# Graph score rows spread by a DRAM round trip instead of TensorE transposes, with a new table of planner aims

## The chip, the cores and the metric

The kernel runs on one core of a Trainium2 chip. The metric is device time in microseconds of the whole launch. PE is TensorE's matmul side and PEld its weight loads, DVE is VectorE, ACT is ScalarE, POOL is GpSimd, and SP is SyncE, which only issues DMAs here.

## The reference, cut to what matters

Sixteen graphs of 1024 nodes with 256 features go through two layers. Layer 0 is attention with 8 heads, masked by the adjacency; layer 1 applies graph attention twice, and then a feed-forward block. The graph attention is the part that the change touches:

```python
def _gat(h, adj, W, a, out_features):
    Wh = h @ W
    Wh1 = Wh @ a[:out_features]              # one score per node (row)
    Wh2 = Wh @ a[out_features:]              # one score per node (column)
    e = leaky_relu(Wh1 + swapaxes(Wh2, 1, 2), 0.2)
    att = softmax(where(adj > 0, e, NEG), axis=1)
    return att @ Wh
```

`e[i, j]` depends on a number of row i and a number of row j alone. The kernel has j on the partitions and i along the free axis, so the 1024 numbers `Wh1[i]` have to stand as a line that is the same on all 128 partitions.

## The kernel before, in words

All in float32. A planner written in the kernel, the class `Order`, decides in which order instructions are issued on each engine. The work is written as threads (generators) that yield the cost of their next instruction in nanoseconds, such as `on(PE=460)` or `load()`; they take and give buffers of counted pools, and wait for and fire events. The planner goes through all threads at build time and puts, of those instructions that could start within 300 ns of the first one, the one with the smallest `aim` next. Aims are due times, computed from two tables of constants: `AIM`, and `EARLY` for the first two graphs, in units of `SLOT`. The order is then fixed: on the chip every engine runs its list strictly in order and waits for semaphores. SP's list of DMAs is such a list too.

The work of one graph b:

- `mask_part` turns the adjacency into a float8 mask; `x_pair`, `qk_part` (L492, L495, L497) and `v_part` (L524) make transposed inputs, queries and keys (stored to DRAM as high and low halves, L504) and values. They are done for graph b+1 while graph b is in its heads. `load_stacks` (L581) loads the queries and keys of a head from DRAM on SP's queue, into two buffers.
- `all_scores` and `weights`: for every head 8 tiles of scores, in pairs. PE writes a pair (L615, four matmuls) into the two PSUM buffers `ps_s`; for each tile ACT scales it (L631), DVE takes the larger of both (L633), which frees the PSUM buffer, ACT takes the exponential (L636), and POOL multiplies by the mask (L640). `join` (L699, DVE) adds tiles for the row sums. `all_values` is the product with the values on PE (L655). Because there are only two `ps_s` buffers, PE's next L615 pair waits for both L633 of the pair before it.
- `rest`: row norms, L792 to L829 in `rows_pair` (projection, norm, then the product L824 that yields the rows of `Wh` and both scores; ACT copies the rows, L827, DVE copies the two scores into the small tile `check`, L829).
- `attention` runs twice per graph, s = 0 and s = 1. `first_half` makes half of the line: four transposes of a score column that is read as if it were repeated over 128 columns (L860), into one of three `misc` PSUM buffers, and two exponentials on ACT (L862, L864) into the tile `first`. Then `attend` makes eight tiles `att` on DVE, each with L877 (product and maximum), L880 (mask and sum) and L883 (reciprocal), and ACT scales a row block by the reciprocal (L885). Every `attend` needs both halves of `first`. The products that follow, L915 for s = 0 (`second_rows`, which gives the rows and scores for s = 1 by L923 and L925) and L940 for s = 1 (`normed_pair`), need all eight `att` tiles.
- `feed_forward`: L980 and L1008 on PE, evacuated by ACT L989 or DVE L986, then norms on DVE (L350, L352, L1019, L1021) and the store of the result. It can be done late, so that the planner uses it to fill PE in the following graph.

All of this is `unshifted_path`. A second path, `general_path`, is branched to at the end only where sums or scores left a safe range, and isn't executed with these inputs.

In the steady part, one graph takes one slot: 32 score pairs with the values, both graph attentions, and the feed-forward of an earlier graph, all interleaved.

Of the kernel before, what the change touches and what calls it, by code (L numbers as in the profile page):

```python
# [9 lines left out]
FT = mybir.dt.float32  # L10
# [4 lines left out]
AF = mybir.ActivationFunctionType  # L15
OP = mybir.AluOpType

ALPHA = 0.2
EPS = 1e-5
H = 8  # L20
P = 128
HALF = 512
# [164 lines left out]
def on(shared=False, delay=0.0, mode=None, **costs):  # L187
    return "on", (costs, shared, delay, mode)
# [6 lines left out]
def wait(event):  # L195
    return "wait", event
# [6 lines left out]
def take(pool):  # L203
    return "take", pool


def give(pool):
    return "give", pool


def start(thread, aim):
    return "start", (thread, aim)


def aim(time, lead):
    return "aim", (time, lead)
# [17 lines left out]
def unshifted_path(  # L234
# [8 lines left out]
    nc = tc.nc  # L243
    B, N, D = x.shape
    NT = N // P
# [6 lines left out]
    TPH = HALF // P  # L252
# [7 lines left out]
    YW = D + 2  # L260
    NSUM = NT * H + 2 * NT
    NSCORE = 4 * NT
    SLOT = 253e3
    PACE = SLOT / (H * NT // 2)


    AIM = dict(mask0=0.602, x=1.454, x_step=-0.0104, mask=0.9396, mask_step=-0.0101, qk0=0.4907, qk1=1.7441,
               qk_step=-0.0518, v0=0.7416, v1=0.621, v_step=0.0547, rows=-0.079, rows_step=-0.0113, first0=0.2137,
               first1=-0.446, graph0=-0.0793, graph1=0.316, graph_step=0.0481, second=0.7493, second_step=-0.015,
               normed=1.0223, normed_step=-0.0115, ff_wait=(None, 0, 1, 0), ff=(0.5532, 0.1074, 3.6996, 1.0353),  # L270
               ff_step=0.0063, fast0=0.2312, fast1=0.6979, fast15=1.0127, lead=14.8372)

    EARLY = dict(x=2.6481, x_step=-0.1001, mask=0.5019, mask_step=0.0795, qk0=0.7532, qk1=1.2626, qk_step=-0.1325,
                 v0=0.2134, v1=1.5023, v_step=-0.0416, rows=-2.7213, rows_step=-0.3343, first0=-0.8482,
                 first1=-4.695, graph0=0.0441, graph1=-0.9035, graph_step=-0.1073, second=0.463,
                 second_step=0.0554, normed=0.7744, normed_step=0.0342, ff_wait=(None, 0, 1, 0),
                 ff=(2.0875, 0.7055, 1.5112, 0.6358), ff_step=0.0607)

    const = ctx.enter_context(tc.tile_pool(name="const", bufs=1))
    sb = ctx.enter_context(tc.tile_pool(name="sb", bufs=1))  # L280
# [2 lines left out]
    dram = ctx.enter_context(tc.tile_pool(name="dram", bufs=3, space=bass.MemoryType.DRAM))  # L283
# [4 lines left out]
    def share(b, name):  # L288
        return (EARLY if b < 2 else AIM)[name]

    def misc(dtype=FT):
        return psum.tile([P, HALF], dtype, tag=f"misc{work.slot['misc']}", name="ps_m", bufs=1)

    def buf(shape, tag, name, dtype=FT):
        return sb.tile(shape, dtype, tag=tag, name=name, bufs=bufs[tag])


    ident = const.tile([P, P], FT, name="ident")
# [40 lines left out]
    def load(n=1, latency=3500):  # L339

        return on(SP=500 * n, delay=latency)
# [62 lines left out]
    def mask_part(b, t, halves):  # L404

        n = len(halves)
        ints = []
        if b:
            yield take("adj")
        elif halves[0]:  # L410
            yield wait(("mask", b, t, 0))
        for kh in halves:
            yield take("pair")
            ai = buf([P, HALF], "pair", "adj_i", I32)
            ints.append(ai)
            part = adj[b].rearrange("(u p i) k -> u i p k", p=P, i=2)[t // 2, t % 2, :, kh * HALF:(kh + 1) * HALF]
            if b:
                yield pause(1500)
                yield on(ACT=400, delay=3500)
                nc.scalar.dma_start(ai, part)  # L420
            else:
                yield pause(2000)
                yield load()
                nc.sync.dma_start(ai, part)
        yield take("adjb")
        ab = buf([P, 2 * HALF], "adjb", "adj_b", F8)
        for i, ai in enumerate(ints):
            yield on(DVE=336, shared=True)
            nc.vector.tensor_scalar(ab[:, i * HALF:(i + 1) * HALF], ai, 0.0, -1.0,
                                    op0=OP.is_gt, op1=OP.mult, saturate=False)  # L430
            yield give("pair")
        if b:
            yield give("adj")
        yield take("misc")
        pt = misc(BF)
        pairs = ab.bitcast(BF)
        yield on(PE=30 + 140 * n)
        for i in range(2 * n):
            nc.tensor.transpose(pt[:, i * P:(i + 1) * P], pairs[:, i * P:(i + 1) * P], ident_b)
        yield give("adjb")  # L440
        yield on(ACT=46 + 218 * n)
        k0 = 2 * halves[0]
        nc.scalar.copy(masks[b].bitcast(BF).rearrange("p (k q) -> p k q", k=NP)[:, k0:k0 + 2 * n, t * P:(t + 1) * P],
                       pt[:, :2 * n * P].rearrange("p (k q) -> p k q", k=2 * n))
        yield give("misc")
        for kh in halves:
            yield fire(("mask", b, t, kh))

    def make_mask(b, t0):
        yield take("mask")  # L450
        masks[b] = buf([P, NT * N], "mask", "mask", F8)
        parts = [(t, (kh,)) for kh in range(NH) for t in range(NT)] if b == 0 else [(t, (0, 1)) for t in range(NT)]
        for n, (t, halves) in enumerate(parts):
            yield start(mask_part(b, t, halves),
                        t0 + ((share(b - 1, "mask") if b else AIM["mask0"]) + share(b - 1, "mask_step") * n) * SLOT)

# [20 lines left out]
    def qk_part(b, g, o, nh):  # L477

        w = (wq, wk)[o]
        cols = slice(nh * HALF, (nh + 1) * HALF)  # L480
        for u in range(nh * 2, nh * 2 + 2):
            yield wait(("xT", b, u))
        if b:
            yield take("stage")
        yield take("pair")
        yield take("pair")
        yield take("misc")
        pa = misc()
        high, low = (buf([P, HALF], "pair", n) for n in ("high", "low"))
        yield on(PE=1728)  # L490
        for dc in range(DC):
            nc.tensor.matmul(pa, w[:, dc, g * P:(g + 1) * P], xTs[b][:, dc, cols],  # L492
                             start=(dc == 0), stop=(dc == DC - 1))
        yield on(ACT=466)
        nc.scalar.copy(high.bitcast(FR), pa)  # L495
        yield on(DVE=594)
        nc.vector.tensor_tensor(low, pa, high, op=OP.subtract)  # L497
        yield give("misc")
        if (b, g) == (0, 1):

            yield wait(("stack", 0, 0))
        yield load(2)
        for i, part in enumerate((high, low)):
            nc.sync.dma_start(scratch[b, g][o, :, i, cols], part)  # L504
        yield give("pair")
        yield give("pair")
        if b:
            yield give("stage")
        yield fire(("qk", b, g, o, nh))

    def project_qk(b, g, t0):
        scratch[b, g] = dram.tile([2, P, 2, N], FT, name="qk_halves")
        for o in range(2):
            for nh in range(NH):
                yield start(qk_part(b, g, o, nh), t0 + (2 * o + nh) * share(b - 1, "qk_step") * SLOT)

# [20 lines left out]
    def project_v(b, g, t0):  # L537
        yield take("v")
        vs[b, g] = buf([P, NT, G * DH], "v", "v")
        for u in range(NP):  # L540
            yield start(v_part(b, g, u), t0 + share(b - 1, "v_step") * u * SLOT)

# [6 lines left out]
    def project(b, t0):  # L549
        yield take("xT")  # L550
        xTs[b] = buf([P, DC, N], "xT", "xT")
        for u in range(NP):
            yield start(x_pair(b, u), t0 + (share(b - 1, "x") + share(b - 1, "x_step") * u if b else 0.0) * SLOT)
        yield start(make_mask(b, t0), t0 + (0.5 if b else 0.0) * SLOT)
        for g in range(H // G):
# [32 lines left out]
    checks = {}  # L588
    begin = {}

    def pace(b):
        return PACE * {0: AIM["fast0"], 1: AIM["fast1"], B - 1: AIM["fast15"]}.get(b, 1.0)

    def all_scores():
        for b in range(B):
# [4 lines left out]
            for h in range(H):  # L600
                yield wait(("stack", b, h))
                q, kk = stacks[b, h]
                for t in range(NT):
                    due = t0 + (h * NT + t) / 2 * pace(b)
                    if b == 0 or t % 2 == 0:
                        yield aim(due, AIM["lead"] * PACE)
                        for _ in range(2 if b else 1):
# [123 lines left out]
    def scores_of(b, s):  # L731

        c = NSUM + s * 2 * NT
        return checks[b][:, c:c + 2 * NT].rearrange("p (t s) -> p t s", s=2)

    def head_stats(b, q):
        got = yield from stats([hn[b][:, q * TPH + i, :] for i in range(TPH)])
# [112 lines left out]
    def first_half(b, s, nh):  # L850

        first, ac = firsts[b, s], scores_of(b, s)
        cols = slice(nh * HALF, (nh + 1) * HALF)
        for t in range(nh * TPH, (nh + 1) * TPH):
            yield wait(("row", b, s, t))
        yield take("misc")
        pt = misc()
        yield on(PE=460)
        for i in range(TPH):
            nc.tensor.transpose(pt[:, i * P:(i + 1) * P], ac[:, nh * TPH + i, 0:1].to_broadcast([P, P]), ident)  # L860
        yield on(ACT=478)
        nc.scalar.activation(first[:, 0, cols], pt, AF.Exp)  # L862
        yield on(ACT=478)
        nc.scalar.activation(first[:, 1, cols], pt, AF.Exp, scale=ALPHA)  # L864
        yield give("misc")
        yield fire(("first", b, s, nh))

    def attend(b, s, big, rows, j, second, sums):
# [616 lines left out]
```

## Time and profile before

| | |
|---|---|
| times of the runs | 4314.66, 4314.74, 4316.35 us (median 4314.74) |
| profiled execution: its own time, its span | 4317.81 us, 4315.9 us |
| PE busy (share of the span) | 4189.7 us (97%) |
| DVE busy | 3544.8 us (82%) |
| ACT busy | 2942.7 us (68%) |
| POOL busy | 2571.6 us (60%) |
| mean granted TensorE clock | 0.990 |
| DMA traffic | 344.79 MB, 80 GB/s on average |

Busy time is the union of an engine's instructions; the group rows of the profile add up their own instructions, and neighbours on PE overlap because matmuls are pipelined. What ended an idle time is named behind it. A row such as `DVE L633 ... [0.53 <-ACT p L631]` of the timeline says that DVE stood idle for 0.53 us before it, until ACT had done L631.

### The profile page before, as it was taken

The numbers are of one execution on the slowest core, as the hardware profiler recorded it, in microseconds if no ns is written. First come the engines' busy times: TensorE is split into PE (matmuls) and PEld (weight loads), VectorE is DVE, ScalarE is ACT, GpSimd is POOL, SyncE is SP. The second block draws the span as 40 slices with busy tenths as digits, with TensorE's granted clock in tenths as the row PEclk, the third lists the DMA queues.
The fourth block names the chain that finished last, engine by engine and source line by source line (L and its number), as shares of the span: only waits on it lengthen the run. The fifth ranks groups of instructions, "written<-read, shape, count | busy, mean of one in ns | idle before, by whom it ended". The sixth has DMA issues, their size and how long they took to land.

```text
span 4315.9 us, 76274 instructions
## 1 busy us (share of the span) xinstructions
PE 4189.7 (97%) x30027; PEld 3030.3 (70%) x30027; DVE 3544.8 (82%) x5491; ACT 2942.7 (68%) x4362; POOL 2571.6 (60%) x1161
## 2 busy tenths in 40 slices
PE   8788999999999999999999999999999999999999
PEld 4466677677777777777777777777777777777687
DVE  6878878888888887879879788887889879788853
ACT  6756677777767677776776767677776776767632
POOL 5846467664757656574664757646575674747700
PEclk9999999999999999999999999999999999999999
DMA  6413223322232322323232222322323222222100
GB/s 188 125 54 99 69 76 87 91 72 86 74 94 67 96 84 68 90 71 89 84 84 81 79 81 79 91 73 81 91 74 89 81 84 84 74 79 57 30 20 21
DMA packets 156282, 344.79 MB, mean 80 GB/s; under 512 B 21750, under 2 KB 24332, under 8 KB 155916
## 3 DMA queue, kind: packets, MB, share of 16 engines
q1 hardware_dynamic: 112140, 260.13, 21.0%
q10 hardware_dynamic: 43776, 79.71, 6.6%
q8 instruction: 239, 3.92, 0.4%
q14 instruction: 127, 1.04, 0.1%
HBM read 239.09 MB, written 100.66 MB: 79 GB/s over the span
## 4 chain that ended last, share of the span: by engine, by line
PE 82%; DVE 11%; ACT 3%; POOL 1%; DMA 1%; issue 1%; SPq 0%; ACTq 0%; POOLq 0%; DVEq 0%
PE ps_a L655 17%; PE ps_s L615 11%; PE ps_m L915 10%; PE ps_m L980 9%; PE ps_m L940 9%; PE ps_m L1008 7%; PE ps_m L492 4%; DVE p L633 3%; PE ps_m L792 3%; PE ps_m L824 3%; PE ps_m L795 3%; PE ps_m L524 2%; PE ps_m L372 2%; DVE p L699 2%; POOL p L640 1%; DVE att L880 1%
## 5 line engine op out<-in xcount | busy, mean ns | idle before, releaser
L640 POOL TENSOR_TENSOR p<-p,mask 128x1024 f32<-128x1024 f32 x1024 | 2471.1, 2431 | 1425.5 <-ACT p L636 1044.1
L633 DVE TENSOR_TENSOR p<-p,ps_s 128x1024 f32<-128x1024 f32 x1024 | 1211.3, 1213 | 251.2 <-ACT p L631 248.1
L636 ACT ACTIVATE p<-p 128x1024 f32<-128x1024 f32 x1024 | 1082.2, 1059 | 302.3 <-DVE p L633 276.7
L631 ACT ACTIVATE p<-ps_s 128x1024 f32<-128x1024 f32 x1006 | 986.3, 1021 | 345.2 <-PE ps_s L615 283.0
L615 PE MATMUL ps_s<-qs,ks 128*128 128x512 f32 x2048 | 658.7, 437 | 30.6 <-DVE p L633 27.0
L655 PE MATMUL ps_a<-p,v 128*32 128x256 f32 x8192 | 561.9, 388 | 24.4 <-POOL p L640 24.3
L615 PEld LDWEIGHTS ps_s<-qs,ks 128*128 128x128 f32 x2048 | 352.6, 190 | 266.1 <-issue 114.8
L940 PE MATMUL ps_m<-y,att 128*128 128x256 f32 x2048 | 481.1, 382 | 12.6 <-ACT y L885 11.1
L915 PE MATMUL ps_m<-y,att 128*128 128x258 f32 x2048 | 477.1, 383 | 14.4 <-ACT y L885 12.9
L980 PE MATMUL ps_m<-rT,wf 128*128 128x256 f32 x2048 | 474.3, 383 | 9.4 <-ACT hid L989 4.3
L1008 PE MATMUL ps_m<-wf,hid 128*128 128x256 f32 x2048 | 475.7, 381 | 0.6 <-DVE hid L986 0.6
L915 PEld LDWEIGHTS ps_m<-y,att 128*128 128x128 f32 x2048 | 385.5, 190 | 89.3 <-ACT y L885 13.8
L980 PEld LDWEIGHTS ps_m<-rT,wf 128*128 128x128 f32 x2048 | 381.0, 190 | 85.9 <-issue 14.3
L699 DVE TENSOR_TENSOR p<-p 128x1024 f32<-128x1024 f32 x256 | 410.5, 1604 | 23.6 <-PE ps_a L655 23.4
L940 PEld LDWEIGHTS ps_m<-y,att 128*128 128x128 f32 x2048 | 378.4, 190 | 71.1 <-ACT y L885 11.3
L1008 PEld LDWEIGHTS ps_m<-wf,hid 128*128 128x128 f32 x2048 | 379.1, 190 | 63.6 <-issue 8.2
L655 PEld LDWEIGHTS ps_a<-p,v 128*32 128x32 f32 x8192 | 209.5, 109 | 289.3 <-issue 130.8
L655 PE MATMUL ps_a<-p,minus_ones 128*32 128x256 f32 x6144 | 405.8, 382 | 1.2 <-DVE p L699 1.2
L877 DVE SCALAR_TENSOR_TENSOR att<-first,second 128x1024 f32<-128x1024 f32 x256 | 359.7, 1405 | 32.4 <-ACT first L864 28.3
L880 DVE SCALAR_TENSOR_TENSOR att<-mask,att 128x1024 f32<-128x1024 fp8e4 x256 | 339.5, 1326 | 5.6
L655 PEld LDWEIGHTS ps_a<-p,minus_ones 128*32 128x32 f32 x6144 | 199.1, 111 | 138.3 <-issue 7.9
L885 ACT ACTIVATE y<-y,check 128x258 f32<-128x258 f32 x256 | 131.1, 512 | 220.4 <-DVE check L883 217.9
(101 smaller groups left out, 4330.0 us busy)
## 6 DMA issues: line engine op xcount, KB each, us to landing
qs<-qk_halves SPq DMA_DIRECT2D x256, 256.0 KB, 4.0
ks<-qk_halves SPq DMA_DIRECT2D x256, 256.0 KB, 5.2
adj_i<-in_adj_dram ACTq DMA_DIRECT2D x240, 256.0 KB, 3.1
qk_halves<-high SPq DMA_DIRECT2D x128, 256.0 KB, 2.8
qk_halves<-low SPq DMA_DIRECT2D x128, 256.0 KB, 3.6
xr<-in_x_dram ACTq DMA_DIRECT2D x64, 256.0 KB, 4.7
x_kept<-x SPq DMA_DIRECT2D x64, 256.0 KB, 2.0
x<-x_kept SPq DMA_DIRECT2D x64, 256.0 KB, 5.1
```

The lines of the kernel that those rows point to most:

```text
L615: nc.tensor.matmul(ps[:, cols], kk[:, t * P:(t + 1) * P], q[:, cols], start=True, stop=True)
L631: nc.scalar.activation(p, ps, AF.Copy, scale=ALPHA)
L633: nc.vector.tensor_tensor(p, p, ps, op=OP.max)
L636: nc.scalar.activation(p, p, AF.Exp)
L640: nc.gpsimd.tensor_tensor(p, p, mask_of(b, t), op=OP.mult)
L655: nc.tensor.matmul(acc[i * DH:(i + 1) * DH, at:at + QN].rearrange("d (t r) -> d t r", r=DH), w, p.rearrange("k (t i r) -> k i t r", i=4, r ...
L699: nc.vector.tensor_tensor(ps[to], ps[to], ps[by], op=OP.add)
L880: nc.vector.scalar_tensor_tensor(e, mask_of(b, j), -1.0, e, op0=OP.mult, op1=OP.mult, accum_out=sums[:, j:j + 1])
L915: nc.tensor.matmul(pa[:, cols:cols + width], big[:, j, i * P:(i + 1) * P], rows[:, j, :width], start=(j == 0), stop=(j == NT - 1))
L940: nc.tensor.matmul(pa[:, i * D:(i + 1) * D], big[:, j, t * P:(t + 1) * P], y2[:, j, :D], start=(j == 0), stop=False)
L980: nc.tensor.matmul(pa[:, i * 2 * P:(i + 1) * 2 * P], wf1[:, dc, hc * P:(hc + 1) * P], rT[:, dc, :], start=(dc == 0), stop=(dc == DC - 1))
L1008: nc.tensor.matmul(pa[:, i * D:(i + 1) * D], hid[hc // 2][:, hc % 2, i * P:(i + 1) * P], wf2[:, hc, :], start=(hc == 0), stop=False)
```

## The change

The four transposes and their PSUM buffer are gone. SP stores the four score columns of a half, 128 partitions x 4 numbers, to a line of 512 numbers in DRAM, and then loads this line back with a partition step of zero, so that every one of 128 partitions receives it in a tile `raw` of the `pair` pool. The exponentials read `raw` in SBUF. In `check` the first and second scores of a graph now lie in two blocks instead of alternating. `SLOT` and nearly all constants of `AIM` and `EARLY` are new, so that the planner puts nearly all instructions of the program in another order. In the changed program, lines from `first_half` on stand three lines lower (L877 is L880 there, and so on); the text keeps the numbers of the kernel before.

```diff
-    SLOT = 253e3
+    SLOT = 251e3
     PACE = SLOT / (H * NT // 2)
-    AIM = dict(mask0=0.602, x=1.454, x_step=-0.0104, mask=0.9396, mask_step=-0.0101, qk0=0.4907, qk1=1.7441,
-               qk_step=-0.0518, v0=0.7416, v1=0.621, v_step=0.0547, rows=-0.079, rows_step=-0.0113, first0=0.2137,
-               first1=-0.446, graph0=-0.0793, graph1=0.316, graph_step=0.0481, second=0.7493, second_step=-0.015,
-               normed=1.0223, normed_step=-0.0115, ff_wait=(None, 0, 1, 0), ff=(0.5532, 0.1074, 3.6996, 1.0353),
-               ff_step=0.0063, fast0=0.2312, fast1=0.6979, fast15=1.0127, lead=14.8372)
+    AIM = dict(mask0=0.0973, x=3.4713, x_step=0.2368, mask=0.8043, mask_step=-0.0042, qk0=-0.2028, qk1=3.8613,
+               qk_step=-0.1291, v0=0.5183, v1=0.0617, v_step=0.1189, rows=-0.9474, rows_step=0.0512, first0=0.1622,
+               first1=-0.0793, graph0=-0.6118, graph1=0.2848, graph_step=0.0401, second=0.5052, second_step=0.0603,
+               normed=1.2995, normed_step=0.0726, ff_wait=(None, 0, 1, 0), ff=(1.133, 0.7743, 3.8606, 0.5991),
+               ff_step=0.258, fast0=0.3229, fast1=0.6862, fast15=0.8129, lead=9.3223)
...
-        return checks[b][:, c:c + 2 * NT].rearrange("p (t s) -> p t s", s=2)
+        return checks[b][:, c:c + 2 * NT].rearrange("p (s t) -> p t s", s=2)
...
-        yield take("misc")
-        pt = misc()
-        yield on(PE=460)
-        for i in range(TPH):
-            nc.tensor.transpose(pt[:, i * P:(i + 1) * P], ac[:, nh * TPH + i, 0:1].to_broadcast([P, P]), ident)
-        yield on(ACT=478)
-        nc.scalar.activation(first[:, 0, cols], pt, AF.Exp)
-        yield on(ACT=478)
-        nc.scalar.activation(first[:, 1, cols], pt, AF.Exp, scale=ALPHA)
-        yield give("misc")
+        line = dram.tile([TPH, P], FT, name="first_line")
+        yield load(latency=2500)
+        nc.sync.dma_start(line.rearrange("t p -> p t"), ac[:, nh * TPH:(nh + 1) * TPH, 0],
+                          allow_slow_non_contiguous=True)
+        yield take("pair")
+        raw = buf([P, HALF], "pair", "raw")
+        yield load()
+        nc.sync.dma_start(raw, bass.AP(tensor=line.tensor, offset=line.offset, ap=[[0, P], [1, HALF]]))
+        yield on(ACT=465)
+        nc.scalar.activation(first[:, 0, cols], raw, AF.Exp)
+        yield on(ACT=465)
+        nc.scalar.activation(first[:, 1, cols], raw, AF.Exp, scale=ALPHA)
+        yield give("pair")
```

The table `EARLY` changes in the same way and is not shown.

More of the change, by code (lines that the diff above doesn't have):

```diff
@@ L262, in unshifted_path @@
     NSCORE = 4 * NT
-    SLOT = 253e3
+    SLOT = 251e3
     PACE = SLOT / (H * NT // 2)
-    AIM = dict(mask0=0.602, x=1.454, x_step=-0.0104, mask=0.9396, mask_step=-0.0101, qk0=0.4907, qk1=1.7441,
-               qk_step=-0.0518, v0=0.7416, v1=0.621, v_step=0.0547, rows=-0.079, rows_step=-0.0113, first0=0.2137,
-               first1=-0.446, graph0=-0.0793, graph1=0.316, graph_step=0.0481, second=0.7493, second_step=-0.015,
-               normed=1.0223, normed_step=-0.0115, ff_wait=(None, 0, 1, 0), ff=(0.5532, 0.1074, 3.6996, 1.0353),
-               ff_step=0.0063, fast0=0.2312, fast1=0.6979, fast15=1.0127, lead=14.8372)
[L273 to L277, printed above, removed]
+    AIM = dict(mask0=0.0973, x=3.4713, x_step=0.2368, mask=0.8043, mask_step=-0.0042, qk0=-0.2028, qk1=3.8613,
[3 more added lines that the diff above has]
+               ff_step=0.258, fast0=0.3229, fast1=0.6862, fast15=0.8129, lead=9.3223)
+    EARLY = dict(x=1.0175, x_step=-0.0658, mask=0.5592, mask_step=0.0737, qk0=1.1297, qk1=1.4913, qk_step=-0.2752,
+                 v0=0.4539, v1=3.6536, v_step=-0.0971, rows=-3.4944, rows_step=-0.1049, first0=-0.0367,
+                 first1=-6.585, graph0=-0.3717, graph1=-1.8154, graph_step=-0.1035, second=0.6069,
+                 second_step=-0.006, normed=1.0065, normed_step=0.0779, ff_wait=(None, 0, 1, 0),
+                 ff=(2.9283, 0.5368, 1.4214, 0.1568), ff_step=0.1386)
     const = ctx.enter_context(tc.tile_pool(name="const", bufs=1))
```

## The prediction

> **What bounds the kernel now.** I read the page first, then the busy times in windows of one slot, then what PE waited for, then the timeline of PE and DVE where graph scores are spread.
>
> ```profile
> span 4315.9 us, 76274 instructions
> PE 4189.7 (97%) x30027; PEld 3030.3 (70%) x30027; DVE 3544.8 (82%) x5491; ACT 2942.7 (68%) x4362; POOL 2571.6 (60%) x1161
> ...
> 1059.46:1319.61 260.15, 258.37 (x1872) 187.95 (x1873) 221.71 (x344) 184.02 (x272) 161.73 (x72) 1.00 0.29 84
> 1319.61:1579.75 260.14, 258.38 (x1873) 187.96 (x1873) 221.61 (x344) 183.96 (x272) 161.47 (x72) 1.00 0.29 82
> ```
>
> The window columns are length, then busy time of PE, PEld, DVE, ACT and POOL, then clock, DMA share and GB/s. A slot lasts 260.14 us and PE works 258.4 of them at full clock: the steady part is PE's. Of PE's 126 idle us, 82 lie before 540 us and 17 after 4000 us. In between PE waits little:
>
> ```profile
> PE ps_a L655 <- POOL p L640: 6.6, 11, 0.6
> PE ps_s L615 <- DVE p L633: 5.9, 13, 1.1
> PE ps_m L792 <- ACT mask L443: 3.7, 11, 0.3
> ```
>
> But 97% does not say how near the next engine is. DVE does the eight `attend` of a graph in a cluster between two score pairs, and then the next L615 hangs on it (first DVE, then PE, in two clusters of one slot):
>
> ```profile
> 1049.25 1.20 DVE L633 TENSOR_TENSOR p<-p,ps_s 128x1024 f32<-128x1024 f32 x1
> ...
> 1068.35 2.33 DVE L633 TENSOR_TENSOR p<-p,ps_s 128x1024 f32<-128x1024 f32 x2
> ...
> 1184.80 2.33 DVE L633 TENSOR_TENSOR p<-p,ps_s 128x1024 f32<-128x1024 f32 x2
> ...
> 1044.22 1.19 PE L615 MATMUL ps_s<-qs,ks 128*128 128x512 f32 x4
> ...
> 1071.91 1.49 PE L615 MATMUL ps_s<-qs,ks 128*128 128x512 f32 x4
> ...
> 1187.73 1.21 PE L615 MATMUL ps_s<-qs,ks 128*128 128x512 f32 x4
> ```
>
> DVE ends its pairs at 1070.6 and 1187.1, PE starts the next ones at 1071.9 and 1187.7. The clusters clear PE by 1.3 and 0.7 us.
>
> **What is removed.** 64 halves of four transposes.
>
> ```profile
> 1039.18 0.65 PE L860 MATMUL ps_m<-ident,check 128*128 128x128 f32 x4
> 1039.67 3.62 PE L980 MATMUL ps_m<-rT,wf 128*128 128x256 f32 x16
> ...
> L860 PE MATMUL ps_m<-ident,check 128*128 128x128 f32 x256 | 36.8, 274 | 1.0 <-DVE check L829 0.6 <-DVE low L497 0.3
> ```
>
> The group says 36.8 us, but matmuls overlap their neighbours; from start to start a half costs 0.49 us. 64 x 0.485 = **31.0 us**, or 1.95 per slot. The freed `misc` buffer costs and brings nothing: hardly a PE wait is for one. The exponentials stay 128, now from SBUF: 600 ns from PSUM now, and L636 (SBUF, 1059 ns) against L631 (PSUM, 1021) says some tens of ns either way, below ACT's 32% idle: 0.
>
> **What is added.** 64 stores and 64 loads on SP's queue, 0.33 to 0.47 us of issue each, some 50 us of a queue that waits over 1200 us for PE alone; 17 MB more on DMA engines that are busy 0.29. Taken at 0. The latency counts:
>
> ```profile
> adj_i<-in_adj_dram ACTq DMA_DIRECT2D x240, 256.0 KB, 3.1
> ...
> x_kept<-x SPq DMA_DIRECT2D x64, 256.0 KB, 2.0
> x<-x_kept SPq DMA_DIRECT2D x64, 256.0 KB, 5.1
> ...
> setup<-in_L_gnn_a_dram SPq DMA_DIRECT2D x4, 1.0 KB, 4.7
> ```
>
> The load (256 KB) I take at 3.5 us (3.1 to 5.1). The store writes 512 single numbers. The nearest row is the last one, four DMAs of 256 single numbers: issued 0.5 us apart they land 4.5 to 4.9 us after issue, behind large loads. So one adds at most (0.5 + 0.13) us, 512 numbers 1.3 us: 2.0 + 1.3 = **3.3 us**. The Trainium skill speaks against it: "DMA: Bandwidth & Descriptors", Rules for kernel authors, has a strided last dim lowered to one descriptor per element and advises against it, and its section Bandwidth gives about 10.5 ns per packet; one element per packet, one after another, would be 512 x 10.5 ns = 5.4 us, an estimate: 7.4 us for the store. The four small loads, at under 2.5 ns per number, disagree with that price, so 3.3 stands and 7.4 is the upper end (2.0 the lower).
>
> From the score copy L925 to the exponential that is two store issues (0.8), 3.3, a load issue behind the wait (0.6), 3.5: **8.2 us**, against some 2.5 before (in the last graph L925 ends at 4193.25 and the last L862 starts at 4195.8). What covers it, by the changed program's instruction order in a steady slot: between the last score copy of s = 1 and its exponentials lie two score pairs of PE time, 9.9 us; at s = 0 three pairs, 17 us. Hidden at 3.3, with 1.7 us to spare. Without this cover it would be 5.7 us twice a slot. SP waits for the store in front of each load; behind stand the next head's L581 loads and L504 stores. A head lasts 32.5 us and has two buffers, so 5 us there cost 0.
>
> **What is moved.** The order of all engines is new, so I add up the new clusters with durations from the trace: one `attend` 2.65 us where POOL is quiet (4142.54 to 4145.21), L633 and L699 1.13, L497 0.6; on PE eight L980 or L1008 1.73, four L492 1.7, four L615 1.1.
> - s = 0: the DVE cluster has 7 `attend` (18.55), two L633, L699, three L497, and norms, 27.2 us; one more `attend`, norms and an exponential of the line on ACT now stand ahead of it between the L633 of its first pair, so that it starts 7.5 us after that pair's L615 (6.2 before); 0.5 for POOL on the shared operands (1.2 to 1.8 in the two clusters before). 35.2. PE has 33.0 us of work from that L615 to the one that needs it: 48 L980 and 32 L1008 (17.3 together), 12 L492 (5.1), 72 L655 (4.1), 16 L915 (3.5), two L615 pairs, small ones. **PE waits 2.2 us.**
> - s = 1: four exponentials and L495 stand on ACT in front, so the first `attend` starts 8.5 us after L615; 7.5 of them, two L497, L699 and two L633 take 24.5; 33.0 in all. PE has 32.7. With a hop, **0.5 us**.
>
> DVE's 5.9 us of L615 waits go. Net: 13 slots x 2.7 = 35.1, less 5.9.
>
> The first graph has little filler. There PE waited 12.9 and 11.1 us for L885 before L915 and L940. New sums from the last row: `att` complete after 39.8 and 41.1 us (chain, interleaved L633 and eight `attend`), PE work 28.9 and 25.2: waits 10.9 and 15.9, **+3 us**. The last graph:
>
> ```profile
> 4193.09 0.16 DVE L925 COPY check<-ps_m 128x2 f32<-128x2 f32 x1 [3.33 <-ACT y L923]
> ...
> 4192.48 1.89 PE L980 MATMUL ps_m<-rT,wf 128*128 128x256 f32 x8
> ...
> 4216.94 3.62 PE L940 MATMUL ps_m<-y,att 128*128 128x256 f32 x16
> ```
>
> The last scores come at 4193, PE has 24.5 us of other work until L940. In the new order 19.9, and 3.0 until the first tile's eighth row; the line (9.9 with the x1 loads ahead of it on SP), eight `attend` (21.2) and L885 (0.7) take 31.8: **+9 us**. For s = 0 the same sum is even (31.2 against 31.3).
>
> Sum against the profiled execution's own 4317.8: - 31.0 - 5.9 + 35.1 + 3 + 9 = 4328.0; the median of the runs is 3.1 lower: **4325**.
>
> **The rivals.**
> - *The clusters hold.* If DVE's clusters end 3 us earlier than my sums, PE stays full: 4314.7 - 31 + 12 = 4296, and 4284 if the tail holds too. For it: PE waits of 0.6% now, and my cluster sums carry 2 us of doubt each. Against: DVE has the same work, packed closer; the old clusters cleared by only 1.3 and 0.7. It decides at the L633 that ends a cluster: before or after PE's 33 us.
> - *The store is slow.* At 7.4 us the line of s = 1 comes 4.1 - 1.7 = 2.4 us late behind ACT's exponentials, 13 x 2.4 = 31, and 14 at both ends: 4370. For it: 4-byte writes to DRAM are not in the trace. Against: the four small loads.
> - That the transposes stay is excluded: the changed program's order has none of the 256, and as many other matmuls.
>
> **How the numbers follow.** Chances: gain eaten by clusters and tail 0.45 (its own range 4308 to 4342), clusters hold 0.31, slow store 0.24. What a measurement can tell from no change is about 0.2%, 8.6 us: below 4306 is faster (nearly all of the second case, 0.29), 4306 to 4323 the same (0.22, mostly the lower half of the first), above slower (0.49). The range 4286 to 4366 leaves out the best of the second case and the worse half of the third.
>
> **What would show it.** Right: no L860; PE busy near 4155; a slot of 258.5 to 261; PE waits L615 <- L633 and L655 <- L699 of 1 to 3 us once a slot, and ACT L885 ahead of the last L940 with some 9 us; the store landing in 3 to 4 us. Wrong: slots of 258 with no such waits (the second case); or ACT waiting on `raw` for over 1 us per slot (the third).

## The result, and the profile after

| | before | after |
|---|---|---|
| median of the runs | 4314.74 us | 4521.66 us (4517.04 to 4532.51) |
| ratio | | 1.0483, interval 1.0468 to 1.0497 |
| span of the profiled execution | 4315.9 us | 4519.9 us |
| PE busy, idle | 4189.7, 126 us | 4225.9, 294 us |

The forecast was 4325, with a range up to 4366. The direction was right; the time lies far outside. From the page after:

```profile
span 4519.9 us, 75963 instructions
PE 4225.9 (93%) x29771; PEld 3023.1 (67%) x29771; DVE 3581.1 (79%) x5463; ACT 2946.7 (65%) x4390; POOL 2496.6 (55%) x1161
...
PE 56%; DVE 23%; DMA 11%; ACT 6%; issue 2%; POOL 1%; SPq 1%; ACTq 0%; DVEq 0%; POOLq 0%
```

256 matmuls are gone, and PE is busy for 36 us *more*. The last line is the chain of work that ended last: before, it was PE for 82% and DMA for 1%. Two slots after, by windows (length, PE, PEld, DVE, ACT, POOL, clock, DMA share, GB/s):

```profile
1081.70:1352.60 270.90, 259.14 (x1838) 185.83 (x1838) 218.09 (x333) 185.20 (x275) 154.82 (x73) 0.98 0.34 82
1352.60:1623.50 270.90, 258.84 (x1844) 186.02 (x1846) 220.79 (x338) 184.01 (x273) 155.43 (x72) 0.99 0.32 82
```

A slot lasts 270.9 us, 10.8 more than before. The waits say for what (total, times, longest):

```profile
PE ps_s L615 <- DVE p L633: 50.2, 55, 4.9
...
SPq L863 <- DMA first_line<-check: 357.5, 48, 15.3
...
ACT first L865 <- DMA raw<-first_line: 100.2, 29, 11.3
```

L863 is the load of the line and L865 the first exponential: ACT stands for 100 us in front of a line that is not there, the sign named for the third case. Followed through one slot, the chain runs from the last score copy L928 through the line into the `attend`:

```profile
1191.55 0.04 DVE check L928
1191.59 0.02 issue
1191.61 10.97 DMA first_line<-check
1202.58 0.02 issue
1202.60 0.02 SPq L863
1202.61 0.03 issue
1202.64 4.18 DMA raw<-first_line
1206.82 0.02 issue
1206.85 0.03 ACT first L865
1206.87 0.51 issue
1207.38 0.62 ACT first L867
1208.01 0.03 issue
1208.03 1.30 DVE att L880
```

The store takes 11.0 us where 3.3 was taken; the load takes 4.2 (3.5 was taken). From score copy to the last exponential it is 15.8 us, not 8.2. Elsewhere in the chain a load of the line alone takes 9 to 14 us (12 of its 22 pieces); 11 of these 12 begin within 2.3 us of the issue of another store. PE also pays after such a stall (timeline of PE):

```profile
1093.38 2.35 PE L615 MATMUL ps_s<-qs,ks 128*128 128x512 f32 x4 [2.59 <-DVE p L633]
...
1095.95 5.47 PE L1011 MATMUL ps_m<-wf,hid 128*128 128x256 f32 x16
```

Undisturbed, these two take 1.2 and 3.6 us. Before the stall the granted clock is 1.00, after it 0.53 (windows, columns as above):

```profile
1060.00:1090.00 30.00, 29.92 (x220) 21.67 (x222) 17.98 (x45) 18.22 (x37) 8.98 (x4) 1.00 0.31 46
1094.00:1100.00 6.00, 6.00 (x17) 4.41 (x16) 3.64 (x5) 5.41 (x6) 5.51 (x4) 0.53 1.18 105
```

Over the kernel the mean granted clock falls from 0.990 to 0.977. At the old clock, the busy time after would be 4225.9 x 0.977 / 0.990 = 4170 us, an estimate from these figures: some 55 us of it are the lower clock.

### The profile page after: what moved, and what is told of

It is laid out like the page before. It is cut to its first block, busy times and chain, and to the rows that moved or that the text cites. A ratio compares the mean times of both kernels' runs of the same rounds, so it can differ in the third digit from the quotient of the medians.

```text
span 4519.9 us, 75963 instructions
## 1 busy us (share of the span) xinstructions
PE 4225.9 (93%) x29771; PEld 3023.1 (67%) x29771; DVE 3581.1 (79%) x5463; ACT 2946.7 (65%) x4390; POOL 2496.6 (55%) x1161
## 4 chain that ended last, share of the span: by engine, by line
PE 56%; DVE 23%; DMA 11%; ACT 6%; issue 2%; POOL 1%; SPq 1%; ACTq 0%; DVEq 0%; POOLq 0%
PE ps_a L655 13%; PE ps_m L918 9%; PE ps_m L943 9%; PE ps_s L615 8%; DVE att L883 5%; DVE att L880 5%; DVE p L633 5%; DMA first_line<-check 4%; DMA raw<-first_line 4%; PE ps_m L1011 3%; PE ps_m L792 3%; PE ps_m L795 3%; ACT p L631 2%; PE ps_m L983 2%; PE ps_m L492 2%
## 5 line engine op out<-in xcount | busy, mean ns | idle before, releaser
L640 POOL TENSOR_TENSOR p<-p,mask 128x1024 f32<-128x1024 f32 x1024 | 2416.2, 2377 | 1697.0 <-ACT p L636 1328.8
L633 DVE TENSOR_TENSOR p<-p,ps_s 128x1024 f32<-128x1024 f32 x1024 | 1212.9, 1213 | 281.0 <-ACT p L631 275.5
L615 PE MATMUL ps_s<-qs,ks 128*128 128x512 f32 x2048 | 655.1, 436 | 54.6 <-DVE p L633 50.2
L615 PEld LDWEIGHTS ps_s<-qs,ks 128*128 128x128 f32 x2048 | 349.8, 191 | 280.4 <-issue 95.1
L943 PE MATMUL ps_m<-y,att 128*128 128x256 f32 x2048 | 490.9, 384 | 28.4 <-ACT y L888 28.4
L983 PE MATMUL ps_m<-rT,wf 128*128 128x256 f32 x2048 | 484.4, 384 | 32.2 <-ACT hid L992 17.5
L699 DVE TENSOR_TENSOR p<-p 128x1024 f32<-128x1024 f32 x256 | 428.1, 1672 | 46.0 <-PE ps_a L655 41.1
L1011 PEld LDWEIGHTS ps_m<-wf,hid 128*128 128x128 f32 x2048 | 390.0, 194 | 86.1 <-ACT xT L330 16.7
L880 DVE SCALAR_TENSOR_TENSOR att<-first,second 128x1024 f32<-128x1024 f32 x256 | 338.3, 1322 | 21.8 <-ACT first L867 21.8
```

The lines of the kernel that those rows point to most:

```text
L615: nc.tensor.matmul(ps[:, cols], kk[:, t * P:(t + 1) * P], q[:, cols], start=True, stop=True)
L633: nc.vector.tensor_tensor(p, p, ps, op=OP.max)
L640: nc.gpsimd.tensor_tensor(p, p, mask_of(b, t), op=OP.mult)
L880: nc.vector.scalar_tensor_tensor(e, first[:, 0, :], second[:, j:j + 1], first[:, 1, :], op0=OP.mult, op1=OP.max)
L943: nc.tensor.matmul(pa[:, i * D:(i + 1) * D], big[:, j, t * P:(t + 1) * P], y2[:, j, :D], start=(j == 0), stop=False)
L983: nc.tensor.matmul(pa[:, i * 2 * P:(i + 1) * 2 * P], wf1[:, dc, hc * P:(hc + 1) * P], rT[:, dc, :], start=(dc == 0), stop=(dc == DC - 1))
```

## The experiments

In three theories: the line comes too late (latency); the new tables pack the work badly, by whatever route the line comes (order); the store holds up its neighbours (queue). All ratios are against the kernel before on the same chip.

### One order, with and without the line

**e1: the changed order, row for row, without store and load.**

```diff
-        nc.sync.dma_start(line..., ac[...])
-        nc.sync.dma_start(raw, <line, repeated>)
-        nc.scalar.activation(first[:, 0, cols], raw, AF.Exp)
+        nc.scalar.activation(first[:, 0, cols], wf1[:, 0, :HALF], AF.Exp)
```

> The changed kernel's order of all engines, instruction for instruction, but neither the store of the scores nor the load of the line: the exponentials of a half read the tile wf1 instead, which is there from the start, so the line itself is left out. Latency theory (the line arrives 5 to 10 us later than its cover): PE busy falls back to about 4155 and the time to 4290 to 4330. Order theory (the new tables pack DVE's clusters too closely, by whatever route the line comes): the time stays above 4450. Queue theory (the store holds up its neighbours on the queue): as latency, 4290 to 4330.

Measured: 4391.4 (1.0178, 1.0161 to 1.0195). Outside the ranges of all three theories: 130 us of the loss are the line, and 77 are there without it. PE's busy time is 4173.5 us in e1, so that 52 us of the line's cost are added busy time (at a mean clock of 0.977 against 0.985 in e1); the rest, some 81 us by the table below, is idle time.

**e9: the order of the kernel before, row for row, with the transposes left out.**

```diff
-            nc.tensor.transpose(pt[...], ac[...].to_broadcast([P, P]), ident)
-        nc.scalar.activation(first[:, 0, cols], pt, AF.Exp)
+        nc.scalar.activation(first[:, 0, cols], wf1[:, 0, :HALF], AF.Exp)
```

> The order of the kernel before on every engine, row for row, with only the transposes left out (the exponentials read wf1, so the line itself is left out). It measures the first term of the sum by itself. If a half costs PE 0.485 us from start to start and nothing else ends later: 4314 - 31 = 4281 to 4287. If DVE's clusters end just in time in the old order, part of it is lost: 4288 to 4305.

Measured: 4316.6 (1.0003, 0.9994 to 1.0012). Above both ranges: taking the transposes away brings nothing. This is the first term of my sum, measured by itself. The slot, its PE waits from 1000 to 4000 us, and the chain that ended last:

```profile
1063.38:1323.86 260.48, 257.13 (x1856) 186.27 (x1856) 223.29 (x344) 183.53 (x272) 160.17 (x72) 1.00 0.29 84
```
```profile
PE ps_m L980 <- ACT hid L989: 10.4, 11, 1.0
PE ps_s L615 <- DVE p L633: 9.5, 24, 0.6
```
```profile
PE 71%; DVE 19%; ACT 6%; issue 2%; POOL 1%; DMA 0%; SPq 0%; ACTq 0%; POOLq 0%; DVEq 0%
```

PE's busy time in the slot is 1.2 us shorter (258.4 before), and the slot is 0.3 us longer. PE comes earlier to the end of a DVE cluster and waits there. The chain, followed through a slot, now leaves PE for ACT's four exponentials and DVE's `attend` from 1153 to 1182 us, and comes back to it so:

```profile
1182.20 0.18 DVE check L883
...
1182.39 0.02 ACT y L885
...
1182.81 0.46 ACT hid L989
...
1183.32 3.72 PE ps_m L980 x16
```

The cluster reaches PE by way of ACT: L989, which empties the `misc` buffer that L980 needs, stands behind L885 in ACT's list, and L885 waits for DVE. This wait of 10.4 us is not among those of the kernel before; L615's wait for L633, the one that the prediction looked at, was 4.8 there and is 9.5 here.

The loss so far, by medians: transposes out +2, new order +75 (e1 against e9), line +130 (after against e1), together 207. PE's idle time by stretch, from the windows of each kernel, shows where:

| PE idle, us | before | e9 | e1 | after |
|---|---|---|---|---|
| 0 to 540 us | 82 | 83 | 97 | 109 |
| 540 to 4000 us | 27 | 49 | 80 | 133 |
| after 4000 us | 17 | 19 | 36 | 52 |

### Why the transposes bring nothing

**e13: the kernel before without L877; e14: e9 without L877.** Both keep the old order.

```diff
-        nc.vector.scalar_tensor_tensor(e, first[:, 0, :], second[:, j:j + 1], first[:, 1, :], ...)
-        nc.vector.scalar_tensor_tensor(e, mask_of(b, j), -1.0, e, ...)
+        nc.vector.scalar_tensor_tensor(e, mask_of(b, j), -1.0, first[:, 0, :], ...)
```

> The kernel before, order kept on every engine, transposes kept; only L877 is left out on DVE (L880 then reads first instead of att), about 1.3 us of each attend and 10 us of each of the two clusters in a slot. If PE alone bounds the kernel: 4308 to 4316, as PE's work is the same. If DVE's clusters alone bound it: 4150 to 4250. If both bound it, within a us of each other, PE holds it: 4300 to 4316.

> The same without L877 and without the transposes (the exponentials read wf1, so the line is left out too), in the order of the kernel before. If DVE's clusters were what kept the 31 us of the transposes from being gained, PE now gains them in full: 4275 to 4290. If something else holds the slot (evacuations of misc buffers by ACT, POOL's products): 4300 to 4316, as without L877 alone.

Measured: e13 4282.5 (0.992, 0.9904 to 0.9937), e14 4253.6 (0.9859, 0.9843 to 0.9875). With DVE relieved, the same 256 transposes are worth 4282.5 - 4253.6 = 28.9 us, near the 31 of the sum; without that, nothing. From 1000 to 2000 us:

```profile
1000.00:2000.00 1000.00, 986.27 (x7097) 712.69 (x7096) 853.46 (x1307) 706.52 (x1049) 618.50 (x278) 1.00 0.28 82
```
```profile
1000.00:2000.00 1000.00, 992.96 (x7201) 720.90 (x7194) 775.34 (x1246) 708.03 (x1033) 604.34 (x281) 1.00 0.29 82
```

The first is e9, the second e14: PE is idle 13.7 us per 1000 beside a full DVE cluster, and 7.0 beside a lighter one, near the 6.2 of the kernel before. L980's wait for L989 is gone in e14. The expectation for e13 was wrong, though, and that for e14 (4275 to 4290) with it: e13 gained 33 us although PE's work is the same. Its PE idle time is 26 us shorter before 540 us, where there is little filler, and unchanged in the steady part. So the steady slot had two bounds at nearly the same length, PE and the clusters, and the start had one, DVE.

**e18: the changed order without a line (e1), without L877** (the same cut).

> The changed order without a line (4391) and without L877 in its attend (L880 there; the mask step reads first). In the old order the same cut brought 4316.6 to 4253.6, 63 us. If the 75 us of the new order are DVE's clusters: it gains more than that, 65 to 140 us, down to 4255 to 4325. If they are waits elsewhere (evacuations of misc buffers outside the clusters, start and end): it gains less than 63 us, and stays above 4330.

Measured: 4351.0 (1.0082, 1.0066 to 1.0099), a gain of 40, under the 63 of the old order; PE's idle time from 540 to 4000 us falls from 80 to 74 us only. So in the steady part the clusters aren't what the new order costs. The PE waits of e1 and of e18, from 1000 to 4000 us (e1's lines are 5 lower than those after, e18's 7):

```profile
PE ps_m L792 <- DVE hT L389: 16.6, 11, 1.5
PE ps_m L978 <- ACT hid L987: 14.3, 11, 1.3
PE ps_m L1006 <- ACT xT L330: 10.9, 11, 1.1
...
PE ps_s L615 <- DVE p L633: 3.2, 11, 0.3
```
```profile
PE ps_m L792 <- DVE hT L389: 16.6, 11, 1.5
PE ps_m L976 <- ACT hid L985: 14.2, 11, 1.3
PE ps_m L1004 <- ACT xT L330: 10.7, 11, 1.0
```

They are the same with and without L877, 11 times each, once a slot, and nearly all on `ps_m`: PE wants a `misc` buffer that ACT or DVE has not emptied yet. The L615 wait that the prediction put its 2.2 + 0.5 us on is 0.3.

### What in the line costs 130 us

**e3 and e11: the changed order and its waits, with the store in 128 runs of 16 bytes, and in 256 of 8** (the numbers then stand in another order in the line).

```diff
-        nc.sync.dma_start(line.rearrange("t p -> p t"), ac[:, nh * TPH:(nh + 1) * TPH, 0], ...)
+        nc.sync.dma_start(<line, ap=[[TPH, P], [1, TPH]]>, ac[:, nh * TPH:(nh + 1) * TPH, 0])      # e3
+        nc.sync.dma_start(<line, ap=[[2, P], [2 * P, 2], [1, 2]]>, ac[...].rearrange("p (u v) -> p u v", v=2))   # e11
```

> The changed kernel's order and waits; the store writes each partition's 4 numbers as one run of 16 bytes, 128 pieces instead of 512 (the numbers then stand in another order in the line). If the store's cost goes by the number of pieces, it falls from 9 to 10 us to 3 to 4 us, the line comes some 6 us earlier and the time is 4320 to 4390. If a write to DRAM has a fixed delay of that size whatever its pieces, the store stays at 8 us or more and the time at 4480 to 4530. Order theory: no change, 4500 to 4530.

> The changed kernel's order and waits; the store in 256 pieces of 8 bytes (the numbers of the line in another order). Between 512 pieces (9.7 us, 4522) and 128 (1.4 us, 4390). If the time of a store goes by its pieces: some 4 to 5 us, and the line just fits its cover of 9.9 us: 4395 to 4440. If pieces under some size are each as dear as single numbers: 4500 or more.

Measured: e3 4390.1 (1.0176, 1.0159 to 1.0193), e11 4389.7 (1.018, 1.0163 to 1.0197): both as without a line, and e11 better than its range (4395 to 4440). A DRAM round trip as such is hidden; the 130 us are the price of single numbers. The DMA view of e3 and then of e11 gives the median us from issue to landing in its last column:

```profile
raw<-first_line SPq DMA_DIRECT2D x64, 256.0 KB, 4.4
...
first_line<-check SPq DMA_DIRECT2D x64, 2.0 KB, 1.4
```
```profile
raw<-first_line SPq DMA_DIRECT2D x64, 256.0 KB, 5.3
...
first_line<-check SPq DMA_DIRECT2D x64, 2.0 KB, 3.9
```

For the changed kernel the view gives no landing. From the issue of a store to the issue of the load that waits for it, the median of 64 is 10.6 us there.

**e2, e17 and e8: which wait is it?** In e2 the load reads numbers of x and so does not wait for the store; in e17 it is also issued by ACT, on another queue; in e8 the load is as it was and the store goes to ACT's queue.

```diff
-        nc.sync.dma_start(raw, <line, repeated>)
+        nc.sync.dma_start(raw, <x[b], repeated>)        # e2
+        nc.scalar.dma_start(raw, <x[b], repeated>)      # e17
-        nc.sync.dma_start(line.rearrange("t p -> p t"), ...)
+        nc.scalar.dma_start(line.rearrange("t p -> p t"), ...)      # e8
```

> The changed kernel's order; the store of the scores stays, but the load reads 512 numbers of the input x instead of the stored line, so that it does not wait for the store (what is left out is the dependence of the line on the scores). Latency theory: what is left of the delay is the load alone, 4 to 5 us against a cover of 9.9 us, so 4290 to 4350. Queue theory (the store's single numbers block the descriptors of everything behind them): the load and x_kept, xr, ks still land late, and the time stays above 4450. Order theory: above 4450.

> The changed kernel's order; the store of single numbers stays on SP's queue, and the load reads 512 numbers of x (what is left out is the dependence of the line on the scores) and is issued by ACT, on the queue of adj_i and xr, so that it neither waits for the store nor stands behind it. If the 130 us are the late line: near the order without a line, 4391 plus the 7 us of unread stores and some for ACT's issues: 4395 to 4420. If the store slows all transfers of this order: 4450 to 4510, as with the load on SP's queue (4503).

> The changed kernel with its orders of PE and DVE; only the store of single numbers is issued by ACT instead of SP, so that it stands on ACT's queue (with the loads of adj_i and xr), while the load of the line and all other DMAs stay on SP's. Queue theory (a slow store delays what stands behind it in its own queue): SP's neighbours are free, the load still waits for the store: 4420 to 4490. If the single numbers delay all queues alike: 4500 to 4540. If the store itself is quick on another queue (landing in under 4 us): 4390 to 4410.

Measured: e2 4503.2 (1.0438, 1.042 to 1.0455), e17 4527.5 (1.0494, 1.0476 to 1.0511), e8 4557.1 (1.0563, 1.0547 to 1.0579). e8 and e17 are slower than all their ranges. Neither the wait nor the shared queue is needed. In e17's timeline the store of a graph's second half is issued at about 1191 us, and this is the load of the first half:

```profile
1194.31 0.33 ACTq L863 DMA_DIRECT2D raw<-in_x_dram  x1
...
1206.08 0.63 ACT L865 ACTIVATE first<-raw 128x512 f32<-128x512 f32 x1 [4.84 <-DMA raw<-in_x_dram]
```

A load on another queue, waiting for nothing, lands 11.75 us after its issue (4.4 in the median of e3, with its store in runs of 16 bytes). If the store takes its 10.6 us, it is over at about 1202, and the load comes some 4 us after that, as if it stood behind it. The window in between and one after it, in the columns of the slots above:

```profile
1194.50:1201.50 7.00, 7.00 (x49) 4.68 (x51) 5.97 (x8) 5.19 (x6) 6.33 (x3) 1.00 0.50 31
...
1203.00:1205.00 2.00, 2.00 (x10) 1.69 (x10) 0.00 (x0) 0.00 (x0) 1.48 (x1) 1.00 0.93 344
```

In the first the DMA engines are busy 0.50 for 31 GB/s, where a slot before had 84 GB/s at 0.29; in the second they move 344 GB/s. The packet records of this trace add something: the store's pieces all start between 1192.1 and 1192.5 us and take some 8 ns each, but the first packet of ACT's queue starts at 1203.3. So the pieces are not worked off slowly one after another; for some 10 us behind them, little moves. It is so in the changed kernel too: in the median its 512 pieces start within 0.5 us, and from 6 to 10 us after a store's issue the other transfers move 23 GB/s on average (93 in the 3 us ahead of it). This fits the Trainium skill's "Trainium Kernel Development and Optimization", Key Constraints: SP's, ACT's and POOL's queues run on the same 16 DMA engines. That they interleave, as it also says, is not seen in this stretch. What inside the engines holds the load back no run shows. e8's expectation of free neighbours fell with it.

**e15 and e16: the store alone, in the kernel before.** Transposes and order are kept; 64 stores of single numbers are added at the transposes, read by nobody, on SP's queue (e15) or ACT's (e16).

```diff
+        nc.sync.dma_start(line.rearrange("t p -> p t"), ac[...], allow_slow_non_contiguous=True)   # e16: nc.scalar
```

> The kernel before with its transposes and its order; 64 stores of 512 single numbers are added on SP's queue, at the transposes, and nothing reads what they write. If the store costs only by the wait for the line: 4312 to 4325. If it holds up the transfers behind it on the queue (loads of heads, stores of queries and keys) by some 8 us: 4345 to 4450.

> As before, with the 64 added stores issued by ACT, on its queue, and nothing reads them. SP's queue has no store in it. If a slow store holds up its own queue alone: 4312 to 4335 (adj_i and xr have time to spare, and ACT pays 0.38 us an issue). If it delays the transfers of all queues: within 30 us of the run with the stores on SP's queue.

Measured: e15 4322.9 (1.0021, 1.0014 to 1.0028), e16 4331.2 (1.0033, 1.0022 to 1.0044), some 7 and 15 us. PE's busy share from 1000 to 4000 us stays at 99.2% in e15. Where what it delays has cover, the store is nearly free. So it isn't the slow stretch of the DMA engines by itself that costs, but what has no cover for it. In the changed kernel's chain that is the line above all: 197 us of it are stores and 186 us loads of the line, against some 80 us of other large transfers. How the 130 us divide between the late line and other late transfers was not measured: the changed order with a store that nobody reads was not run.

### Does the change need its order, and do the tables carry over?

**e10: the old order with a 16-byte store and load in the place of each group of transposes**, nothing moved to cover them (the numbers of the line in another order).

```diff
-            nc.tensor.transpose(pt[...], ...)
+        nc.sync.dma_start(<line, ap=[[TPH, P], [1, TPH]]>, ac[...])
+        nc.sync.dma_start(first[:, 1, cols], <line, repeated>)
```

> The order of the kernel before on every engine, with a store in runs of 16 bytes and the load in the place of each group of transposes (the numbers of the line then stand in another order; the load goes into the tile first, since there is no room for a buffer). No instruction is moved to cover it: the line takes about 1.4 + 0.6 + 4.4 us where the order leaves some 2.5. If ACT's wait of about 4 us a half goes to PE in full: 64 x 4 = 250, 4530. If two halves share a wait and half of it is covered by what PE still has to do: 4330 to 4420. If the order has room for it after all: under 4300.

Measured: 4527.3 (1.0499, 1.0482 to 1.0517): even this line (in the median, store 4.4 us and load 3.4) costs 211 us over e9 where nothing is moved, in line with the dearest of the three cases; ACT waits 209 us for it. A line by this route needs a new order.

**e4 to e7: tables and instructions crossed.** e4 has the new tables with the transposes, e5 the old tables without a line, e6 the old tables with the single-number store, e7 the old tables with the 16-byte store and a strided read of `raw` that restores the order of the numbers. The planner makes its own order in each; the diffs are those shown, and the tables swapped.

> The new tables and SLOT, with the four transposes into PSUM of the kernel before in place of store and load; the planner makes its own order from that. Latency theory: 4315 to 4360, near the kernel before, with PE busy near 4190. Order theory: 4450 or more.

> SLOT, AIM and EARLY of the kernel before, without transposes and without store and load; the exponentials read the tile wf1, so the line itself is left out. The planner makes its order from that. If the new tables are what costs the 77 us that the changed order still has without a line, this gives 4280 to 4300 (31 us of transposes gone and PE full). If the old tables too can't fill PE once the transposes are away (PE then waits for evacuations or for DVE's clusters), 4310 to 4350.

> The store of 512 single numbers and the load as in the changed kernel, with SLOT, AIM and EARLY of the kernel before. Store theory (9 to 10 us for the single numbers, and what stands behind them on the queue late): slower than the run without a line by 60 to 150 us, 4350 to 4440. If only the changed order is short of cover, and the old tables leave room for a line that comes 15 us later: within 15 us of the run without a line.

> SLOT, AIM and EARLY of the kernel before; the store in 128 runs of 16 bytes (the line then has its numbers in the order partition, tile), the load as it is, and both exponentials put them in order with a strided read of raw. If the piece size is the whole cost of the line, within 10 us of the run without a line, and faster than the kernel before if that one is: 4285 to 4310. If ACT pays for a read with a stride of 16 bytes, its exponentials show it (over 700 ns instead of 620) and the time goes up by less than 10 us.

Measured: 4423.6 (1.0255), 4366.3 (1.0124), 4635.5 (1.0748) and 4526.9 (1.0494), each within 0.002 either way. All four expectations missed. e5 and e9 do the same work: planned anew with the old tables they take 4366, in the old order 4317. The old table is fitted to its own set of instructions; used for this other one, it costs 50 us before anything else is counted. So these four don't tell line and order apart; the runs with a fixed order do. The new tables do suit the line better than the old ones (4522 against 4635).

**e12: the changed order, 16-byte store, and a strided write of the exponentials**, so that it computes all that the changed kernel does.

```diff
-        nc.scalar.activation(first[:, 0, cols], raw, AF.Exp)
+        nc.scalar.activation(first[:, 0, cols].rearrange("q (t p) -> q p t", p=P), raw.rearrange("q (p t) -> q p t", t=TPH), AF.Exp)
```

> The changed kernel's order; the store in runs of 16 bytes, and the exponentials put the numbers in order by a strided write into first (contiguous read). If a strided write costs ACT nothing: 4390 as with the contiguous one. If it is as slow as the strided read (1145 ns instead of 620): 128 x 0.53 = 67 us of ACT, of which a part reaches PE: 4395 to 4440.

Measured: 4437.7 (1.0289, 1.0272 to 1.0307), 84 us better than the changed kernel and 123 short of the one before. The strided write costs as much as e7's strided read (e12's line, then e7's):

```profile
L865 ACT ACTIVATE first<-raw 128x512 f32<-128x512 f32 x64 | 72.0, 1125 | 0.3 <-issue 0.3
```
```profile
L865 ACT ACTIVATE first<-raw 128x512 f32<-128x512 f32 x64 | 73.3, 1146 | 0.0
```

No version that does all the work beat the kernel before. e9 says why, for the old order: without less work on DVE as well, there is nothing to gain. Whether other tables would do better was not tried.

## Why the prediction was wrong, point by point

The sum had three parts. Without the transposes: -31 forecast, +2 measured (e9). What the new order moves: 35.1 - 5.9 + 3 + 9 = +41 forecast, +75 measured (e1 against e9). The line: 0 forecast, as hidden behind its cover, +130 measured (after against e1). The largest miss is the last, and it rests on the size of the store. That the forecast had the right sign is partly luck: it came from clusters, and these are not what cost.

- **"256 transposes, 31.0 us."** The size was right (28.9 from e13 to e14), the place was not: e9 shows 0, with an interval of -3 to +5 us. The prediction had part of the reason in hand, clusters that clear PE by 1.3 and 0.7 us, and charged the clusters only for what the new order adds. These gaps were read at L615, and together (2.0 us) they would have left room for the 1.95 us of a slot; the wait that ends last in e9 is another, L980 for ACT's L989 behind the same cluster (10.4 us of the 18.5 by which PE's idle time from 1000 to 4000 us grows). DVE was the second bound, as e13 and e14 show.
- **"Store 3.3 us", "7.4 the upper end".** This step failed most: 10.6 in the median, 11.0 in the chain shown. The row it was sized by, four small loads into SBUF, says nothing of a store of single numbers to DRAM. The Trainium skill's "DMA: Bandwidth & Descriptors", Rules for kernel authors, advises to rearrange a strided last dim; the trace agrees (10.6 against 1.4 us in runs of 16 bytes), and I weighed it away. Its price per packet (section Bandwidth, about 10.5 ns, measured on loads into SBUF) agrees with the packet records, 9.9 ns a piece, but it isn't what a landing costs: the pieces start within half a microsecond, not one after another, and the landing takes 3.0 us at least for 256 of them (e11) and 7.8 at least for 512 (from the issue of a store to that of its load, among the changed kernel's 64).
- **"The load 3.5 us".** 4.2 alone after the store, but 11.75 when it is issued beside a store (e17), and 9 to 14 in 12 pieces of the changed kernel's chain.
- **"9.9 us of cover" at s = 1.** Right: in e1, where nothing is late, the last score copy is at 1158.55 and the exponentials of the halves start at 1168.67 and 1170.17, 10.1 and 11.6 us later. It was the chain that was mis-sized, not the cover. The third rival had the mechanism and too low a price.
- **"5 us there cost 0" on SP's queue.** 7 us in the old order (e15). In the changed one SP waits 357 us for its stores, and not only the line comes late: pieces of the chain that last 10 to 14 us are loads of keys and of xr too.
- **"The freed misc buffer costs and brings nothing."** Nearly true of the kernel before: some 6 of the 21 us that PE is idle from 1000 to 4000 us are waits for one. But in e9 the wait that is added is (L980 for L989), and in the new order `misc` buffers are behind 5 of some 6 us of PE waits a slot.
- **Clusters, 35.1 - 5.9 = +29 in the steady part.** e1 against e9 has PE idle for 32 us more there. The size agrees by chance: the waits named (L615 behind L633) are 0.3 a slot, and L877 taken out leaves the real ones as they are (e18).
- **Start +3, tail +9.** Without a line 14 and 17 us (e1 against e9, PE idle), with it 25 and 33 (after against e9).
- **Exponentials at 0.** Right: 615 to 625 ns on average against 593 to 600.

## What to carry to other kernels

A busy share of 97% did not name the bound alone, as DVE's clusters ended within about a microsecond of PE: before an instruction's time is counted as gained, look at what the next wait on that engine would be, or take the instruction out in a fixed order and time it. A DMA of single numbers is priced by a row that has single numbers in the same direction, and here its delay reached transfers issued beside it, on another queue too. A planner's constants belong to one set of instructions; compare a change in a fixed order, or the planner's new order is measured with it.

## What was not expected of the hardware

- Stores of 2 KB to DRAM landed in 1.4 us (e3, e12) in 128 pieces of 16 bytes, in 3.0 (median 3.9) in 256 of 8, and in 7.8 (median 10.6, from issue to the issue of the load behind it) in 512 of 4: the smallest pieces cost more than in proportion, although the pieces themselves start within half a microsecond. In e10, where a load and a second store stand close by, the 128 pieces took 4.4 in the median.
- During a store of single numbers, a load on another queue landed late too (11.75 us against 4.4), and its first packet started only 9 us after its issue.
- After a stall of 2.6 us in the changed kernel, PE's granted clock was 0.53 over 6 us.
- ACT's exponential over 512 elements in SBUF took 615 to 625 ns contiguous, and 1125 to 1146 with a stride of 16 bytes on the read side or 512 on the write side. The Trainium skill's "SBUF — State Buffer", Door 1: The DMA port swizzle, has lines of 16 bytes and a penalty for each access that crosses to a new one; the read agrees with it.
